# One list of events for both products of a graph layer, across its batch norm

## The chip, the cores and the metric

The kernel runs on one core of one Trainium2 chip. The metric is the device time of an execution in microseconds; the time before is the median of five executions, 1886.87 us (1885.16 to 1887.32). One further execution was taken with the profiler; it took 1887.02 us, of which the profile's span is 1885.1 us.

## The reference

Four graph layers follow each other on `x` of 128 x 64 x 256 (batch, nodes, features). Each is `x + layer(relu(layernorm(x)))`. The change is in layer 1:

```python
def _L1_gnn_ref(features, A, W1, b1, g1, be1, W2, b2, g2, be2):
    def _batchnorm(x, gamma, beta):
        mu = jnp.mean(x, axis=0)
        var = jnp.var(x, axis=0)
        return (x - mu) * jax.lax.rsqrt(var + EPS) * gamma + beta
    ...
    agg = jnp.einsum('nm,bmd->bnd', A_hat, features)
    x = agg.reshape(-1, d)
    h = jax.nn.relu(_batchnorm(x @ W1.T + b1, g1, be1))
    out = h @ W2.T + b2
    out = _batchnorm(out, g2, be2)
    return out.reshape(b, n, -1)
```

`W1` takes 256 features to 512, `W2` takes 512 back to 256. A batch norm's mean and variance run over all 8192 rows (128 x 64). So no channel of `h` is known before the first product is done for all rows of that channel.

## The kernel before

**Tiling.** Channels lie on the 128 partitions, rows on the free axis. The 8192 rows are cut into 16 tiles of 512 (`NS = 16`), which are worked on in 8 pairs. The 512 channels of `h` are four chunks of 128, numbered 0 to 3. A tile's chunks 0 and 1 lie in buffers called `hS` or `hT`, chunks 2 and 3 in buffers called `z`; `zslot(s, c)` gives the place of tile `s`, chunk `c`.

**Seven products for eight.** A 2 x 2 block product is done with seven block products (Strassen's way). For this a pair's four blocks b11, b21 (first tile) and b12, b22 (second tile) are used as they are and in differences T1, T2, T4, and a third one written over b12 (called T3 here). Products 1 to 7 are collected in three PSUM banks a, b and c; for instance `product("a", 4)` multiplies by T4 and adds into bank a. A bank is then evicted by ACT (with the bias) or added by DVE to what stands in SBUF already. Bank a is read off step by step, after each of products 1, 6, 7 and 4, which are added into it in this order.

**The first product** (`half`, matmul at L905) is done once for each pair and each half `g` of the output: half 0 makes chunks 0 and 1, half 1 makes chunks 2 and 3. Its order is written out by hand: each step is put into a list with a due time (`at(t, ...)`), the list is sorted, and the steps are issued in that order. All engines work off their own part of this order, first come first. Beside it run the preparation of later tiles (transposes L541, layer norm statistics L564 to L572, aggregation L585, sums L810). `evict` is L910, `add` L913, `stats` (the batch norm's partial statistics) L916. PSUM is split into a pool "gates" of five banks for the product and "rest" of three for the preparation.

**The batch norm's coefficients** (`bn_coeffs`, L857 to L863) are worked out for two chunks at once after each half of the last pair: DVE aggregates the statistics (L857) and adds epsilon (L859), POOL takes the power -1/2 (L860), and DVE does two multiplications and a subtraction (L861 to L863).

**The second product** (`second_product`, matmul at L1015) has a list of its own, sorted and issued after all of the first product. Each pair has 14 matmuls of the program: seven products with `k` = 0 (chunks 0 and 1) and `k` = 1 (chunks 2 and 3), both added into the same bank. In the trace each such matmul has two records. ACT applies the scale, shift and ReLU to each block (L991; four of the first pair's operations are on DVE, L987 and L989), DVE makes the sums of `k` = 0 and POOL those of `k` = 1 (L999 to L1005, both on DVE for the first pair), ACT evicts (L1019), DVE adds (L1022) and takes the second batch norm's statistics (L1028). All eight banks are one pool again. Between the two lists stand the closing of the preparation's memory and seven loads for later layers on SP's queue (L90).

Of the kernel before, what the change touches and what calls it, by code (L numbers as in the profile page):

```python
# [9 lines left out]
F32 = mybir.dt.float32  # L10
AF = mybir.ActivationFunctionType
ALU = mybir.AluOpType
AX = mybir.AxisListType

P = 128
# [5 lines left out]
def kernel(ctx: ExitStack, tc: tile.TileContext, a: dict, out: bass.AP):  # L21
# [60 lines left out]
    def bank(pool="psum"):  # L82
        return banks[pool][1].tile([P, 512], F32, tag="ps", name="ps")
# [4 lines left out]
    def load_const(name, src, shape, pool=const, queue=nc.sync):  # L88
        t = pool.tile(shape, F32, tag=name, name=name)
        queue.dma_start(t, src)  # L90
        return t
# [12 lines left out]
    nc.gpsimd.memset(ones, 1.0)  # L104
    mhalf = const.tile([P, 8], F32, tag="mhalf", name="mhalf")
    nc.gpsimd.memset(mhalf, -0.5)

    def block_diag(name, src):
        t = first.tile([P, P], F32, tag=name, name=name)
# [489 lines left out]
    def at(t, fn, *args):  # L599
        events.append((t, len(events), fn, args))  # L600
# [251 lines left out]
    def bn_coeffs(pool, co, stats, c0, c1, prm, name):  # L852
# [9 lines left out]
        nc.vector.tensor_mul(shift, mv[:, :, 0], scale)  # L862
        nc.vector.tensor_sub(shift, prm[:, 2, c0:c1], shift)  # L863

    co1 = const.tile([P, 3, HC], F32, tag="co1", name="co1")
    co2 = const.tile([P, 3, KC], F32, tag="co2", name="co2")

# [3 lines left out]
    with tc.tile_pool(name="pz", bufs=1, reuse_waits="tile") as pz:  # L871
# [13 lines left out]

        new_banks(gates=5, rest=3)
        GATE = 8.7
        events = []

        def at(t, fn, *args):  # L890
# [2 lines left out]
        def half(i, g):  # L893
            t0, r = GATE * (2 * i + g), {}
            z = {(n, o): zslot(2 * i + n, 2 * g + o) for n in range(2) for o in range(2)}

            def product(name, j):
                new = name not in r
                if new:
                    r[name] = bank("gates")  # L900
                (b11, b21), (b12, b22) = ([firsts[2 * i + n]["ag"][:, c, :] for c in range(KC)]
                                          for n in range(2))
                t1, t2, t4 = firsts[0]["t"]
                x_ = (b11, b21, b22, t4, t1, t2, b12)[j - 1]
                nc.tensor.matmul(r[name], con["w1"][:, OF[j], g, :], x_, start=new,  # L905
                                 stop=(name, j) in (("a", 4), ("b", 3), ("c", 2)), skip_group_check=True)

            def evict(n, o, name):
                m = 2 * g + o
                nc.scalar.activation(z[n, o], r[name], AF.Identity, bias=con["bn1"][:, 0, m : m + 1])  # L910

            def add(n, o, name):
                nc.vector.tensor_add(z[n, o], z[n, o], r[name])  # L913

            def stats(n, o):
                nc.vector.bn_stats(st1[:, 2 * g + o, 2 * i + n, :], z[n, o])  # L916

            for t, name, j in ((0, "c", 2), (1.72, "a", 1), (3.46, "b", 5), (4.32, "a", 6),
                               (6.07, "b", 3), (6.93, "a", 7), (GATE + 0.86, "a", 4)):
                at(t0 + t, product, name, j)  # L920
            for t, fn, n, o, name in ((2.75, evict, 0, 0, "a"), (3.5, add, 0, 0, "c"),
                                      (4.5, evict, 1, 1, "b"), (5.35, evict, 1, 0, "a"),
                                      (7.1, add, 1, 0, "b"), (7.95, add, 1, 1, "a"),
                                      (GATE + 1.9, evict, 0, 1, "a")):
                at(t0 + t, fn, n, o, name)
            for t, n, o in ((5.5, 0, 0), (9.0, 1, 0), (9.7, 1, 1), (GATE + 2.9, 0, 1)):
                at(t0 + t, stats, n, o)
            if i == NS // 2 - 1:
                at(t0 + GATE + 3, bn_coeffs, lns, co1, st1, 2 * g, 2 * g + 2, con["bn1"], "bn1")

        for i in range(NS // 2):
            for g in range(2):
# [22 lines left out]
                at(t2 + (1.7, 2.3, 4.2, 4.8)[q], f.stats, q)  # L955
            at(t2 + 5.4, f.root)

        for _, _, fn, args in sorted(events, key=lambda e: e[:2]):
            fn(*args)
        new_banks(psum=8)  # L960
        front.close()
        last.close()
        late = ctx.enter_context(tc.tile_pool(name="late", bufs=1, side="right", reuse_waits="tile"))
        adj4 = load_const("adj4", parts_d, [P, 4, P], late)
        adj3, smask = adj4[:, 0:3, :], adj4[:, 3, :]
        wl2 = [weight(f"wl2_{k}", a["W"][k], late) for k in range(3)]
        bl2 = row_bcast("bl2", a["bias"], D, late)
        wqk = late.tile([P, KC, D], F32, tag="wqk", name="wqk")
        aqk = late.tile([P, 7, P], F32, tag="aqk", name="aqk")
        wvo = late.tile([P, KC, D], F32, tag="wvo", name="wvo")  # L970
        wqkv = weight("wqkv", a["Wqkv"], late)
        wo = weight("wo", a["Wo"], late)

        events = []

        def second_product(i, tp):


            t0 = 7.0 * i
            tt, banks = {}, {}  # L980

            def z(n, c):
                return zslot(2 * i + n, c)

            def relu(n, c):
                if i == 0 and n == 1 and c % 2 == 0:
                    nc.vector.tensor_scalar(z(n, c), z(n, c), co1[:, 0, c : c + 1],  # L987
                                            co1[:, 1, c : c + 1], op0=ALU.mult, op1=ALU.add)
                    nc.vector.tensor_scalar_max(z(n, c), z(n, c), 0.0)  # L989
                else:  # L990
                    nc.scalar.activation(z(n, c), z(n, c), AF.Relu, bias=co1[:, 1, c : c + 1],  # L991
                                         scale=co1[:, 0, c : c + 1])

            def sums(name, k, engine):
                if name != "T3" and name not in tt:
                    tt[name] = tp.tile([P, 2, SUP], F32, tag=name, name=name)
                b11, b21, b12, b22 = (z(n, 2 * k + c) for n in range(2) for c in range(2))
                if name == "T1":
                    engine.tensor_sub(tt["T1"][:, k], b12, b11)  # L999
                elif name == "T2":  # L1000
                    engine.tensor_sub(tt["T2"][:, k], b22, tt["T1"][:, k])
                elif name == "T3":
                    engine.tensor_sub(b12, b22, b12)
                else:
                    engine.tensor_sub(tt["T4"][:, k], b21, tt["T2"][:, k])  # L1005

            def product(name, j, ks=(0, 1)):
                new = name not in banks
                if new:
                    banks[name] = bank()  # L1010
                for k in ks:
                    x_ = (z(0, 2 * k), z(0, 2 * k + 1), z(1, 2 * k + 1),
                          *(tt[v][:, k] if v in tt else None for v in ("T4", "T1", "T2")),
                          z(1, 2 * k))[j - 1]
                    nc.tensor.matmul(banks[name], w2[:, OF[j], k, :], x_, start=(new and k == 0),  # L1015
                                     stop=(k == 1), skip_group_check=True)
# [11 lines left out]
                nc.vector.bn_stats(st2[:, o, 2 * i + n, :], y(n, o))  # L1028

            def at(t, fn, *args):  # L1030
                events.append((t0 + t, len(events), fn, args))

            for k, (n, c) in enumerate(((0, 1), (0, 0), (0, 3), (0, 2), (1, 0), (1, 2), (1, 1), (1, 3))):
                at((-6.3, -5.8, -5.3, -4.4, -3.9, -3.4, -2.4, -1.9)[k], relu, n, c)
            for k, engine in enumerate((nc.vector, nc.gpsimd if i else nc.vector)):
                for name, t in (("T1", -2.8), ("T2", 0.1), ("T3", 0.6), ("T4", 1.6)):
                    at(t, sums, name, k, engine)
            for t, name, j in ((0, "c", 2), (1, "a", 1), (3, "b", 5), (5, "a", 6), (9, "a", 7),
                               (11, "b", 3), (13, "a", 4)):
                if i == 0 and t < 2:  # L1040
                    at(t, product, name, j, (0,))
                    at(t + 1.1, product, name, j, (1,))
                else:
                    at(t, product, name, j)
            at(2.2, lambda: evict(y(0, 0), 0, "a"))
            at(3.1, lambda: add(y(0, 0), y(0, 0), "c"))
            at(3.6, stats, 0, 0)
            at(4, lambda: evict(y(1, 1), 1, "b"))
            at(6, lambda: evict(tt["T2"][:, 0], 0, "a"))
            at(10, lambda: add(y(1, 1), y(1, 1), "a"))  # L1050
            at(10.5, stats, 1, 1)
            at(12, lambda: add(y(1, 0), tt["T2"][:, 0], "b"))
            at(12.5, stats, 1, 0)
            at(14.2, lambda: evict(y(0, 1), 1, "a"))
            at(15, stats, 0, 1)

        with tc.tile_pool(name="tp", bufs=2, reuse_waits="tile") as tp:
            for i in range(NS // 2):
                second_product(i, tp)
            for _, _, fn, args in sorted(events, key=lambda e: e[:2]):  # L1060
                fn(*args)
        bn_coeffs(lns, co2, st2, 0, KC, con["bn2"], "bn2")


# [354 lines left out]
```

## Time and profile before

| | |
|---|---|
| median of 5 executions | 1886.87 us |
| the profiled execution | 1887.02 us |
| its span | 1885.1 us |
| PE busy | 1859.7 us (99%) |
| DVE busy | 1137.1 us (60%) |
| ACT busy | 923.2 us (49%) |
| POOL busy | 643.2 us (34%) |

Times within the span are counted from its start. The last pair's first half of the first product begins at 1343.7, the second product ends at 1460.7. Busy time by stretch, in us:

| stretch | length | PE | DVE | ACT | POOL | granted clock |
|---|---|---|---|---|---|---|
| 1343.7 to 1356.7, last pair of the first product | 13.00 | 13.00 | 10.42 | 6.09 | 0.70 | 1.00 |
| 1356.7 to 1372.0, the seam | 15.30 | 11.97 | 13.52 | 10.32 | 1.11 | 0.78 |
| 1372.0 to 1390.0, second product | 18.00 | 18.00 | 15.91 | 15.13 | 12.02 | 1.00 |
| 1390.0 to 1460.9, second product | 70.90 | 70.90 | 51.31 | 39.85 | 29.26 | 1.00 |
| 1460.9 to 1475.0, second batch norm, into layer 2 | 14.10 | 10.17 | 10.98 | 6.51 | 8.29 | 1.00 |

How to read the profile: each engine has rows of instructions with start, duration, line, operation, output and inputs, and in square brackets how long the engine stood idle before and what released it. PEld is the weight load, which runs ahead of the matmul (PE). In the table by stretch of the profile the columns are the stretch, its length, busy time and number of instructions of PE, PEld, DVE, ACT and POOL, then the granted TensorE clock, the share of the DMA engines and GB/s. Where an instruction waits for several things, the profile names the one that came last by its own clock, which can be a neighbour in time rather than the true cause. In a group's row the numbers behind the bar are busy us and mean ns of one instruction.

### The profile page before, as it was taken

Reading aid. Unit: us, or ns where it says so; the run is one execution under the profiler, and the core shown is the slowest. Engines: PE = TensorE matmul, PEld = TensorE weight load, DVE = VectorE, ACT = ScalarE, POOL = GpSimd, SP = SyncE. Lnnn points to the kernel's source line nnn. Section 1 sums busy time; section 2 is a strip of 40 time slices with the busy share of each in tenths; the row PEclk is TensorE's granted clock in tenths of the full one; section 3 lists DMA queues with packets and bytes.
Section 4 is the critical chain, followed back from the end, with each engine's and each line's share of the span. In section 5 each row is a group of like instructions: output and inputs, shape, how many; then the busy total and the mean of one; then the engine's idle time right before and its main releaser. Section 6 shows DMA issues by size and latency. Waiting matters only on the chain.

```text
span 1885.1 us, 19823 instructions
## 1 busy us (share of the span) xinstructions
PE 1859.7 (99%) x7080; PEld 1171.1 (62%) x7080; DVE 1137.1 (60%) x2268; ACT 923.2 (49%) x1591; POOL 643.2 (34%) x527
## 2 busy tenths in 40 slices
PE   8999999999999999999999999999999999999999
PEld 7997444444445666666444444556444788888887
DVE  6775777634546445435633333588787776677774
ACT  6775666534435335433533333478574344433442
POOL 4451422543324442422432222377253312211220
PEclk9999999999999999999999999999999999999999
DMA  5110001000001000000000000233200111111100
GB/s 145 57 57 0 1 1 34 12 1 0 1 0 45 1 0 1 1 1 15 8 0 1 1 0 22 101 112 112 70 1 1 46 45 45 35 46 45 46 23 34
DMA packets 50641, 54.85 MB, mean 29 GB/s; under 512 B 3184, under 2 KB 45936, under 8 KB 50544
## 3 DMA queue, kind: packets, MB, share of 16 engines
q1 hardware_dynamic: 50080, 53.40, 9.1%
q8 instruction: 56, 0.92, 0.2%
q14 instruction: 41, 0.34, 0.1%
q10 hardware_dynamic: 464, 0.20, 0.0%
HBM read 36.55 MB, written 17.04 MB: 28 GB/s over the span
## 4 chain that ended last, share of the span: by engine, by line
PE 94%; DVE 3%; ACT 1%; POOL 1%; DMA 1%; issue 0%; SPq 0%; DVEq 0%; POOLq 0%
PE ps L665 34%; PE ps L671 19%; PE ps L1185 8%; PE ps L1015 5%; PE ps L905 5%; PE ps L1250 3%; PE ps L367 3%; PE ps L357 3%; PE ps L396 2%; PE ps L1226 2%; PE ps L1173 2%; PE ps L1260 2%; PE ps L1291 1%; PE ps L585 1%; PE ps L1198 1%; PE ps L541 1%
## 5 line engine op out<-in xcount | busy, mean ns | idle before, releaser
L687 DVE TENSOR_TENSOR gate<-gate,ps 128x512 f32<-128x512 f32 (+2 forms) x378 | 223.9, 620 | 446.9 <-PE ps L671 367.4
L665 PE MATMUL ps<-tx,wih 128*128 128x512 f32 (+2 forms) x1008 | 446.9, 542 | 2.7 <-ACT gate L690 1.0
L665 PE MATMUL ps<-hT,wih 128*128 128x512 f32 (+2 forms) x756 | 338.5, 541 | 0.0
L690 ACT COPY gate<-ps 128x512 f32<-128x512 f32 (+2 forms) x252 | 134.3, 533 | 378.6 <-PE ps L671 325.4
L665 PEld LDWEIGHTS ps<-tx,wih 128*128 128x128 f32 x1008 | 190.5, 190 | 193.3 <-issue 130.1
L683 ACT ACTIVATE gate<-gate,lbias 128x512 f32<-128x512 f32 (+2 forms) x252 | 216.7, 860 | 160.2 <-DVE gate L687 160.2
L671 PE MATMUL ps<-h,whh 128*128 128x512 f32 (+2 forms) x576 | 256.6, 527 | 0.0
L665 PEld LDWEIGHTS ps<-hT,wih 128*128 128x128 f32 x756 | 143.6, 190 | 141.6 <-issue 79.4
L671 PE MATMUL ps<-th,whh 128*128 128x512 f32 (+2 forms) x432 | 192.4, 527 | 0.0
L710 POOL TENSOR_TENSOR gate<-gate 128x1024 f32<-128x1024 f32 (+2 forms) x36 | 71.9, 2019 | 297.6 <-ACT gate L683 297.6
L1185 PE MATMUL ps<-wl,ag 128*128 128x256 f32 x768 | 172.1, 380 | 0.0
L671 PEld LDWEIGHTS ps<-h,whh 128*128 128x128 f32 x576 | 109.4, 190 | 100.2 <-issue 76.5
L1185 PEld LDWEIGHTS ps<-wl,ag 128*128 128x128 f32 x768 | 143.4, 190 | 20.2 <-ACT ag L1178 1.8
L710 POOL TENSOR_TENSOR cell<-gate 128x1024 f32<-128x1024 f32 (+2 forms) x36 | 79.4, 2227 | 175.2 <-ACT gate L683 175.2
L1141 POOL TENSOR_TENSOR ln_rn<-ln_rn,mhalf 128x4 f32<-128x4 f32 (+1 forms) x33 | 32.8, 993 | 300.8 <-DVE ln_rn L1140 300.3
L671 PEld LDWEIGHTS ps<-th,whh 128*128 128x128 f32 x432 | 82.1, 190 | 75.2 <-issue 57.4
L1148 ACT ACTIVATE h<-x,ln_rn 128x256 f32<-128x256 f32 x128 | 68.2, 593 | 103.0 <-DVE ln_rn L1144 103.0
L710 POOL TENSOR_TENSOR cell<-gate,cell 128x1024 f32<-128x1024 f32 (+2 forms) x32 | 65.2, 2055 | 110.2 <-ACT gate L683 110.2
L690 DVE COPY gate<-ps 128x512 f32<-128x512 f32 (+2 forms) x126 | 78.6, 624 | 20.8 <-PE ps L671 20.8
L715 ACT ACTIVATE gate<-cell 128x1024 f32<-128x1024 f32 (+2 forms) x72 | 68.1, 952 | 27.1 <-POOL cell L710 27.1
L683 ACT ACTIVATE gate<-ps,lbias 128x512 f32<-128x512 f32 (+2 forms) x126 | 79.5, 631 | 3.8 <-PE ps L671 1.0
L627 DVE TENSOR_TENSOR tx<-hT,tx 128x512 f32<-128x512 f32 (+2 forms) x72 | 59.1, 820 | 14.9 <-PE ps L665 10.2
(227 smaller groups left out, 2932.5 us busy)
## 6 DMA issues: line engine op xcount, KB each, us to landing
xt<-in_x_dram SPq DMA_DIRECT2D x30, 512.0 KB, 4.2
x1d<-xt SPq DMA_DIRECT2D x16, 512.0 KB, 3.0
x<-x1d SPq DMA_DIRECT2D x16, 512.0 KB, 5.2
out_dram<-x SPq DMA_DIRECT2D x15, 512.0 KB, 3.0
wih<-in_WihT_dram SPq DMA_DIRECT2D x16, 256.0 KB, 5.0
whh<-in_WhhT_dram SPq DMA_DIRECT2D x12, 256.0 KB, 4.9
xt<-in_x_dram SPq DMA_DIRECT2D x8, 128.0 KB, 4.0
wl<-in_W_dram SPq DMA_DIRECT2D x3, 256.0 KB, 4.3
```

Of the source, the lines that this page charges most:

```text
L627: yield nc.vector.tensor_sub(t[k], *((b[1][0], b[0][0]), (b[1][1], t[0]), (b[1][1], b[1][0]), (b[0][1], t[1 % len(t)]))[k])
L665: nc.tensor.matmul(wide(p_[:, :N]), wih[0][:, OF[k], gi, :], x_, start=first_, stop=(j == 0), skip_group_check=True)
L671: nc.tensor.matmul(p_[:, :N], whh[0][:, OF[k], gi, :], h_, start=False, stop=True, skip_group_check=True)
L683: nc.scalar.activation(to, r[bank_][:, :N] if bank_ else to, fn, bias=lbias[:, l, m : m + 1])
L687: nc.vector.tensor_add(slot(n, hc), slot(n, hc), r[bank_][:, :N])
L690: op(slot(n, hc), r[bank_][:, :N])
L710: fn(*((t["G"] if isinstance(t, dict) and "G" in t else st["c"])[:, n, :, : st["N"]] for t in tiles))
L715: nc.scalar.activation(o_, c, AF.Tanh)
L905: nc.tensor.matmul(r[name], con["w1"][:, OF[j], g, :], x_, start=new, stop=(name, j) in (("a", 4), ("b", 3), ("c", 2)), skip_group_check=True)
L1015: nc.tensor.matmul(banks[name], w2[:, OF[j], k, :], x_, start=(new and k == 0), stop=(k == 1), skip_group_check=True)
L1148: nc.scalar.activation(v[tag][:, q, :], v[src][:, q, :], AF.Relu, bias=v["rn"][:, 1, q : q + 1], scale=v["rn"][:, 0, q : q + 1])
L1185: nc.tensor.matmul(v["W"][:, q, :], v["ag"][:, c, m, ts(2 * k + q, P)], wl2[m][:, c, :], start=(n == 0), stop=(n == 3 * KC - 1))
```

## The change

1. **One list.** Layer 1's second product puts its events into the same list as the first. `emit(B + 18.0)` issues all that is due up to then, `B` being the due time of the last pair's start; then the memory is closed and the seven loads are issued as before, and `emit(1e9)` issues the rest.
2. **Coefficients by chunk.** `bn_coeffs1(c)` works out one chunk: DVE aggregates, POOL does the other five steps on one column (add a new constant `eps`, power, two multiplications, a subtraction). It is issued once for each of the four chunks, each after its last statistics.
3. **Early products.** For pairs 0 and 1 the matmuls of a1, b5 and c2 with `k` = 0, which need only chunks 0 and 1, are issued before those with `k` = 1; they come right behind the first product's last matmul. Their T1 with `k` = 0 lies in a tile `early` that is taken from the preparation's memory. The order of ReLUs, sums and evictions of these two pairs is written out anew. Of pair 0's ReLUs one is on DVE (second tile, chunk 1); the two that were there (second tile, chunks 0 and 2) are on ACT.
4. **Two bank pools.** The pools of five and three banks stay through the second product: even pairs take "rest", odd pairs "gates". The pool of eight is made after it.
5. **Due times** of the last pair of the first product are closer together (its second half starts 6.02 after its first, not 8.7). The order of PE's own matmuls in that pair stays as it was.
6. **Sums.** T3 is made before T2, and T2 is T3 + b11 in place of b22 - T1, the same value up to rounding. For pair 1 the sums with `k` = 1 are on POOL as before; pair 0's stay on DVE.

```diff
+    eps = const.tile([P, 1], F32, tag="eps", name="eps")
+    nc.gpsimd.memset(eps, EPS)
...
+    def bn_coeffs1(c):
+
+        mv = lns.tile([P, 2], F32, tag=f"bn1mv{c}", name="bn1mv", bufs=1)
+        nc.vector.bn_aggr(mv, st1[:, c, :, :].rearrange("p s k -> p (s k)"))
+        scale, shift, v = (co1[:, k, c : c + 1] for k in range(3))
+        nc.gpsimd.tensor_add(v, mv[:, 1:2], eps)
+        nc.gpsimd.tensor_tensor(v, v, mhalf[:, :1], ALU.pow)
+        nc.gpsimd.tensor_mul(scale, v, con["bn1"][:, 1, c : c + 1])
+        nc.gpsimd.tensor_mul(shift, mv[:, 0:1], scale)
+        nc.gpsimd.tensor_sub(shift, con["bn1"][:, 2, c : c + 1], shift)
...
+            end = i == NS // 2 - 1
+            if end:
+                t0 = B + 6.02 * g
+            late_a = 6.1 if g else 6.9
...
-            if i == NS // 2 - 1:
-                at(t0 + GATE + 3, bn_coeffs, lns, co1, st1, 2 * g, 2 * g + 2, con["bn1"], "bn1")
+            if end:
+                at(t0 + (7.9 if g else 7.35), bn_coeffs1, 2 * g)
+                at(t0 + 9.2, bn_coeffs1, 2 * g + 1)
...
-        for _, _, fn, args in sorted(events, key=lambda e: e[:2]):
-            fn(*args)
-        new_banks(psum=8)
...
+            def sum_of(name, k):
+                if name == "T1" and k == 0 and i < 2:
+                    if i == 0 and not early:
+                        e = pb[0].tile([P, Q, D], F32, tag="xt", name="early")
+                        early.append(e.rearrange("p (n q) d -> p n (q d)", n=2))
+                    return early[0][:, i]
+                if name not in tt:
+                    tt[name] = tp[0].tile([P, 2, SUP], F32, tag=name, name=name)
+                return tt[name][:, k]
...
-                elif name == "T2":
-                    engine.tensor_sub(tt["T2"][:, k], b22, tt["T1"][:, k])
...
+                elif name == "T2":
+                    engine.tensor_add(sum_of("T2", k), b12, b11)
...
-                    banks[name] = bank()
+                    banks[name] = bank("gates" if i % 2 else "rest")
...
+            if i < 2:
+
+                for t, name, j in (((12.9, "a", 1), (13.76, "b", 5), (14.6, "c", 2)) if i == 0 else
+                                   ((15.5, "a", 1), (16.3, "c", 2), (17.2, "b", 5))):
+                    at_us(t, product, name, j, (0,))
+                for t, n, c in (((11.0, 0, 0), (11.8, 1, 0), (13.0, 0, 1), (17.0, 0, 2), (17.6, 0, 3),
+                                 (18.5, 1, 2), (19.3, 1, 3)) if i == 0 else
+                                ((14.4, 0, 0), (15.2, 0, 1), (16.0, 1, 0), (20.9, 0, 3), (21.6, 0, 2),
+                                 (23.5, 1, 2), (24.3, 1, 1), (25.1, 1, 3))):
+                    at_us(t, relu, n, c)
+                if i == 0:
+                    at_us(17.4, relu, 1, 1, True)
...
+                for t, name, j in (((18.06, "a", 1), (18.92, "c", 2), (19.78, "b", 5)) if i == 0 else
+                                   ((22.4, "c", 2), (23.2, "a", 1), (25.8, "b", 5))):
+                    at_us(t, product, name, j, (1,))
...
+        for i in range(NS // 2):
+            second_product(i)
+        emit(B + 18.0)
         front.close()
         last.close()
...
+        with tc.tile_pool(name="tp", bufs=2, reuse_waits="tile") as tp_:
+            tp.append(tp_)
+            emit(1e9)
+        new_banks(psum=8)
         bn_coeffs(lns, co2, st2, 0, KC, con["bn2"], "bn2")
```

## The prediction, made before the result was known

> **What bounds the kernel now.** The page first: PE is busy 1859.7 of 1885.1 us, so a change can only win where PE waits or runs slowly. The diff touches the seam of layer 1 where the first product (L905) ends, the batch norm takes its coefficients, and the second product (L1015) begins; so next the chain of waits, in order of time, over that seam:
>
> ```profile
> 1343.85 9.16 PE ps L905 x20
> ...
> 1355.44 5.84 DMA wqkv<-in_Wqkv_dram
> 1361.28 2.91 PE ps L1015 x3
> ```
>
> PE carries both sides, and between them stands a DMA whose data the first second-product matmul doesn't read. Which wait is it really? The timelines of PE and of its weight loads:
>
> ```profile
> 1354.74 2.07 PE L905 MATMUL ps<-ag,w 128*128 128x512 f32 x4
> 1358.66 1.12 PE L905 MATMUL ps<-T,w 128*128 128x512 f32 x2 [1.85 <-DVE z L913]
> 1361.26 3.78 PE L1015 MATMUL ps<-hS,w 128*128 128x512 f32 x4 [1.48 <-DMA wqkv<-in_Wqkv_dram]
> 1364.84 3.18 PE L1015 MATMUL ps<-z,w 128*128 128x512 f32 x4
> 1367.86 3.60 PE L1015 MATMUL ps<-T,w 128*128 128x512 f32 x8
> ...
> 1361.26 0.50 PEld L1015 LDWEIGHTS ps<-hS,w 128*128 128x128 f32 x2 [2.31 <-ACT hS L991]
> ```
>
> The weight load names the true releaser, the ReLU on ACT (the wqkv DMA merely ended then). Eight matmuls in 3.60 us are the normal pace: 0.43 us from one start to the next, two records to one product with one k, so 0.86 us for it. The eight from 1361.28 to 1367.86 took 0.82 each. The stretches say why:
>
> ```profile
> 1356.60:1358.60 2.00, 0.21 (x1) 0.00 (x0) 1.97 (x5) 0.00 (x0) 0.00 (x0) 1.00 0.89 227
> ...
> 1361.20:1363.00 1.80, 1.74 (x2) 0.84 (x3) 1.14 (x4) 0.71 (x2) 0.55 (x1) 0.50 0.47 151
> ...
> 1368.00:1370.00 2.00, 2.00 (x6) 0.75 (x5) 2.00 (x4) 2.00 (x5) 0.00 (x0) 1.00 0.00 0
> ```
>
> The column before the last two is the granted clock: 1.00, then 0.50, then 1.00. The loss at the seam: PE's last ordinary L905 work ends at about 1356.63 (last start 1356.2 plus 0.43); the next 46 records (2 of L905, and the 22 single-k products of the first two pairs) should take 46 x 0.4295 = 19.76 us, but the third pair's first matmul starts at 1383.31: 26.68 us. So **6.92 us are lost**: a wait of 2.03 for a z sum on DVE, one of 1.76 for the ReLU, and 8 x (0.82 - 0.43) = 3.14 at half clock. This is nearly all that the change can win.
>
> DVE shows why the z sum is late:
>
> ```profile
> 1353.51 1.02 DVE L857 BATCH_NORM_AGGREGATE bn1mv<-st 128x2 f32<-128x96 f32 x2
> 1354.56 0.17 DVE L859 TENSOR_SCALAR co<-bn1mv 128x2 f32<-128x2 f32 x1
> 1355.54 0.16 DVE L861 TENSOR_TENSOR co<-co,bn 128x2 f32<-128x2 f32 x1 [0.81 <-POOL co L860]
> ...
> 1357.34 1.27 DVE L913 TENSOR_TENSOR z<-z,ps 128x512 f32<-128x512 f32 x2
> ```
>
> DVE works out the coefficients of the first two channel chunks, standing still for POOL's power, with the sums that PE needs queued behind.
>
> **The change, step by step.** I lay the changed program's order on each engine over the times above. Products are named by bank and number as in the code (a4 = product 4 into a); "pair 0, a1 k0" is one single-k product.
>
> **Coefficients to POOL.** DVE keeps only the four aggregates (0.5 each); per chunk POOL gets five steps on one column. Rows: a small multiply 0.20, a one-column power 0.55, 0.08 between dependent steps:
>
> ```profile
> L572 POOL TENSOR_TENSOR ln_rn<-ln_rn 128x4 f32<-128x4 f32 x16 | 3.3, 206 | 1.3
> L175 POOL TENSOR_TENSOR deg<-deg,mhalf 128x1 f32<-128x1 f32 x1 | 0.5, 546 | 0.0
> ```
>
> One chunk: 4 x 0.20 + 0.55 + 4 x 0.08 = 1.67 us. POOL is otherwise idle here (20.3 us before its first power), so nothing is queued behind. Chunk 0 aggregates by 1352.05, so its coefficients stand at about 1353.8; chunk 1 (1354.05) at 1355.9.
>
> **The last L905 products.** DVE is now free when a7 of the last half is done: sum at 1356.84 (its weight load at 1355.68 plus the 1.16 us of the same step one half earlier), ending 1357.53. a4 starts at 1357.55, not 1358.66. PE waits 0.92 instead of 2.03.
>
> **Early products in the gap.** ACT does three ReLUs (0.80, one per 0.70) from 1355.55, in the 4.19 us in which it stood idle: 1356.35, 1357.06, 1357.77. Behind them on ACT is the eviction of a4, which cannot start before 1358.7: no harm. The first early T1 (DVE, 0.69) ends at 1358.14. So at 1358.41 PE goes straight from a4 into pair 0's a1, b5, c2 with k0, then pair 1's a1, c2, b5 (ReLUs 1360.1 to 1361.5, T1 at 1362.25), until 1363.57. No wait among the six.
>
> **Chunks 2 and 3.** a4's eviction ends 1359.4. Chunk 2's aggregate ends at 1359.8, POOL 1361.55; chunk 3's aggregate at 1360.85, POOL starts at 1361.6. Here DVE runs five operations in a row (a difference, the two-step ReLU, T3, T2) until about 1364.4, and POOL meets them. The trace has this meeting once:
>
> ```profile
> 1226.18 2.49 DVE L635 TENSOR_TENSOR hT<-gate 128x512 f32<-128x512 f32 x4
> 1226.28 1.46 POOL L571 TENSOR_TENSOR ln_rn<-ln_rn,mhalf 128x4 f32<-128x4 f32 x1 [4.97 <-DVE ln_rn L570]
> 1227.82 0.31 POOL L572 TENSOR_TENSOR ln_rn<-ln_rn 128x4 f32<-128x4 f32 x1
> ```
>
> The power took 1.46 where its usual is 1.02, the small one 0.31 for 0.20, and DVE lost nothing. By this row chunk 3 pays 0.44 + 4 x 0.11 = 0.88: ready at 1364.15. The Trainium skill speaks against the change here: "SBUF — State Buffer", section "SBUF: two separate sides", holds that a VectorE operation with two SBUF inputs and a GpSimd operation take one port pair exclusively, the later one blocked for a whole instruction. With strict turns the five steps end at about 1365.7. Floor 1363.3 (no meeting), ceiling 1365.7; I take the row, since it is this very pair of operations.
>
> From there: ReLU of z(0,3) 1364.2 to 1365.0, so pair 0's c2 k1 starts at 1365.05 (PE ready at 1364.43: waits 0.62); ReLU of z(1,2) to 1365.7, T1 to 1366.45, so b5 k1 at 1366.5 (waits 0.60). T1's new wait for pair 1's b5 k0 (they share memory) was over at 1363.8. The next six products find their operands ready (ACT's evictions by 0.4 us). Pair 1's a6 k1 needs T3 and T2 from POOL in turn with DVE: ready 1376.6 against 1376.0, 0.65 waited (between 0 and 0.75: POOL's rows here are 1.27 or 1.72). The third pair starts at 1379.2.
>
> **The clock.** With at most 0.92 idle at once I expect 1.00 throughout; after the second batch norm, at 1460.9 to 1475.0, PE was busy only 10.17 of 14.10 us and the clock stayed 1.00. The skill, "TensorE: Matmul & The Clock Gate", section "What's actually happening", lowers the clock after an idle window of about 3.4 us; our gaps were 2.03 and 1.76 with 0.86 of work between, so by a strict reading the clock should not have fallen, and closing them should not return the 3.14. The row shows that it fell right after them: I follow the row. By the rule alone the gain would be 3.14 less.
>
> **The rest.** The two bank pools: an even pair's a takes the bank that the pair two before leaves with its last DVE sum, three slots of 1.72 earlier; DVE meets those sums within 0.4 us of PE now, so that hides it. T2 from T3 instead of T1 is the same count, later by one DVE step (1.75), with some 8 us before its use. After the last pair the transposes wait for a DVE sum that ended 0.8 us before them in this trace. The one added memset is at the start, where POOL waits anyway. SP's seven loads keep their places and released waits.
>
> **Sum.** Lost after: 0.92 + 0.62 + 0.60 + 0.65 = 2.79, against 6.92: **4.1 us won**. The profiled execution took 1887.02 (span 1885.1 and 1.9 around it), so 1882.9; the median of the runs is 1886.87, so 1882.8.
>
> **Rivals.**
> - *POOL and DVE don't disturb each other*: chunk 3 at 1363.3, one wait of 0.36 in place of 0.62 and 0.60. Gain 5.0 (5.6 if a6 needn't wait): 1881.5. For: power and multiply keep 1.02 and 0.20 in all 15 other places. Against: the row at 1226. Chance 0.20.
> - *Full blocking*, chunk 3 at 1365.7: 1.55 later than by the row, so gain 2.5, 1884.3, within the noise. For: the page, and DVE differences of 1.77 beside POOL. Against: the row. Chance 0.11.
> - *The clock falls all the same*: gain 1.0, 1885.9. Against: 0.92 idle. Chance 0.03.
> - *Slower: POOL's one-column steps are dear.* Four chains of five steps in one queue now gate everything. At 1.0 us a step (the 128x4 power) a chain takes 5.3: chunk 1 at 1362.7 holds ACT's ReLU, behind it the eviction of a4, and chunk 3 comes at 1373.3, 9.1 later than I have it: 5.0 lost, 1891.9. It turns to a loss from about 0.75 us a step, which POOL takes for 256 columns; the 0.20 of four columns speaks against it. Chance 0.06.
>
> **Numbers.** The forecast case has 0.60, its own range 1882.0 to 1883.8. Two in ten left out: 1880.8 to 1885.6. A measurement of this kernel tells about 0.2% (3.8 us) from no change. My case lies just beyond, some 0.8 of it counts as faster, with the first rival 0.68; nearly all of the rest is same.
>
> **What would show it.** Right: a4 at about 1357.5; six L1034 products of the two first pairs between 1358.4 and 1363.6 without a gap; the granted clock 1.00 from 1356 to 1370; L872 to L876 at 0.2 to 0.3 us with a power of 0.55 (up to 1.0 in chunk 3); the third pair's first matmul at about 1379. Wrong: a clock of 0.5, POOL steps of 0.6 or more, PE waits for a bank in later pairs, or a pair period other than 12.04 us.

## The result, and the profile after

The changed kernel takes 1882.82 us (median of 30 executions, 1880.74 to 1883.97); beside it, on the same chip, the kernel before takes 1886.07 us (50 executions, 1884.76 to 1888.06). The ratio taken over all executions is 0.9981, 95% interval 0.9976 to 0.9986; the medians alone differ by **3.25 us**, 0.17%. The profiled execution took 1881.2 us (span 1879.5).

| profiled execution | before | after |
|---|---|---|
| span | 1885.1 | 1879.5 |
| last pair's first matmul of the first product | 1343.69 | 1341.40 |
| third pair's first matmul of the second product | 1383.31 | 1377.66 |
| **between them, "the seam"** (also "the stretch") | **39.62** | **36.26** |
| granted clock from 1356.7 to 1372.0 | 0.78 | 1.00 |

The seam gives 3.36 us, which agrees with the medians. The spans differ by 5.6; the other 2.3 are not the change's. About 0.76 lie in two waits of PE for ACT near 17.6 and 20.6 us, and 1.53 in the granted clock at another place, near 1231 us, to which the last section returns. A second profile of the changed kernel (`after_5`, below) has both again, with a seam of 36.25.

The timeline of PE after the change, in the rows that answer to those shown of before:

```profile
1355.30 1.12 PE L919 MATMUL ps<-T,w 128*128 128x512 f32 x2 [0.78 <-DVE z L927]
1356.27 1.02 PE L1034 MATMUL ps<-hS,w 128*128 128x512 f32 x2
1357.12 1.02 PE L1034 MATMUL ps<-early,w 128*128 128x512 f32 x2
1357.98 2.74 PE L1034 MATMUL ps<-hS,w 128*128 128x512 f32 x6
1360.56 1.02 PE L1034 MATMUL ps<-early,w 128*128 128x512 f32 x2
1361.42 1.02 PE L1034 MATMUL ps<-z,w 128*128 128x512 f32 x2
1363.31 1.12 PE L1034 MATMUL ps<-z,w 128*128 128x512 f32 x2 [0.87 <-ACT z L1002]
1364.74 2.84 PE L1034 MATMUL ps<-T,w 128*128 128x512 f32 x6 [0.31 <-DVE T L1018]
...
1374.98 2.84 PE L1034 MATMUL ps<-T,w 128*128 128x512 f32 x6 [0.39 <-POOL T L1022]
```

The first row is a4. The next four are the six early products, without a gap. Then four waits remain in all: before a4, before pair 0's c2 with `k` = 1 (1363.31), before its b5 (1364.74), and before pair 1's a6 (1374.98). From one start to the next, less 0.86 for each pair of records, they cost 0.95 (from 1354.35, when PE is free), 1.03, 0.57 and 0.55. Another 0.46 goes in small pieces: about 0.1 behind the first, third and fourth wait (a4 to the next start: 0.97 for 0.86), and 0.14 around the matmul at 1370.89, before which the profile names no wait. Together 3.56 us are lost now, where 6.92 were.

The table by stretch, with the clock in the column before the last two:

```profile
1356.70:1372.00 15.30, 14.12 (x33) 5.77 (x32) 11.17 (x18) 11.66 (x17) 5.70 (x12) 1.00 0.17 65
1361.20:1363.00 1.80, 1.24 (x3) 0.19 (x1) 1.13 (x2) 0.56 (x1) 1.13 (x2) 1.00 0.00 0
```

PE is busy 14.12 of 15.30 us here, against 11.97 before, with the full clock throughout. (The changed kernel reaches the seam 2.3 us earlier, so the same times take in a somewhat later part of its work.)

What holds the largest wait, at 1363.31? The chain of waits (start, us, what) shows little but POOL's small steps and gaps of 0.04 to 0.08 between them, then a ReLU:

```profile
1359.45 1.04 POOL co L873
...
1360.56 0.40 POOL co L874
...
1361.03 0.65 POOL co L875
1361.77 0.65 POOL co L876
...
1363.16 0.81 ACT z L1002
```

The steps are those for the coefficients of chunk 3. The ReLU in the chain is the one that T1, and so b5, waits for. PE's wait at 1363.31 ends with the ReLU before it, the first of three in ACT's timeline, which start when POOL is done:

```profile
1362.44 2.22 ACT L1002 ACTIVATE z<-z,co 128x512 f32<-128x512 f32 x3 [2.36 <-POOL co L876]
```

The timelines of POOL, for comparison two of chunk 2's steps and then the last four of chunk 3's, and of DVE at the same time:

```profile
1358.51 0.19 POOL L874 TENSOR_TENSOR co<-co,bn 128x1 f32<-128x1 f32 x1
1358.78 0.19 POOL L875 TENSOR_TENSOR co<-bn1mv,co 128x1 f32<-128x1 f32 x1
...
1359.45 1.03 POOL L873 TENSOR_TENSOR co<-co,mhalf 128x1 f32<-128x1 f32 x1
1360.56 0.39 POOL L874 TENSOR_TENSOR co<-co,bn 128x1 f32<-128x1 f32 x1
1361.03 0.65 POOL L875 TENSOR_TENSOR co<-bn1mv,co 128x1 f32<-128x1 f32 x1
1361.76 0.65 POOL L876 TENSOR_TENSOR co<-bn,co 128x1 f32<-128x1 f32 x1
```

```profile
1359.30 0.69 DVE L1018 TENSOR_TENSOR early<-hS 128x512 f32<-128x512 f32 x1 [0.58 <-ACT hS L1002]
1359.91 0.54 DVE L998 TENSOR_SCALAR hS<-hS,co 128x512 f32<-128x512 f32 x1
1360.48 0.43 DVE L1000 TENSOR_SCALAR hS<-hS 128x512 f32<-128x512 f32 x1
1360.94 0.69 DVE L1020 TENSOR_TENSOR hS<-hS 128x512 f32<-128x512 f32 x1
1361.67 0.69 DVE L1022 TENSOR_TENSOR T<-hS 128x512 f32<-128x512 f32 x1
```

Add start and duration in both. L874 on POOL ends at 1360.95, DVE's L1000 at 1360.91. L875 ends at 1361.68, DVE's L1020 at 1361.63. L876 ends at 1362.41, DVE's L1022 at 1362.36. Each small step ends 0.04 to 0.05 after the DVE operation that was running when it began. Whether that is a rule is tested below.

### The profile page after: what moved, and what is told of

The parts are those of the page before. It is cut to its first block, busy times and chain, and to the rows that moved or that the text cites. A ratio compares the mean times of both kernels' runs of the same rounds, so it can differ in the third digit from the quotient of the medians.

```text
span 1879.5 us, 19837 instructions
## 1 busy us (share of the span) xinstructions
PE 1855.6 (99%) x7080; PEld 1169.4 (62%) x7080; DVE 1129.4 (60%) x2258; ACT 923.9 (49%) x1592; POOL 647.0 (34%) x546
## 4 chain that ended last, share of the span: by engine, by line
PE 93%; DVE 3%; POOL 1%; ACT 1%; issue 1%; DMA 0%; ACTq 0%; DVEq 0%; SPq 0%; POOLq 0%
PE ps L667 34%; PE ps L673 19%; PE ps L1256 8%; PE ps L919 4%; PE ps L1034 4%; PE ps L359 3%; PE ps L369 3%; PE ps L1321 3%; PE ps L398 2%; PE ps L1244 2%; PE ps L1297 2%; PE ps L1331 2%; PE ps L1362 1%; PE ps L587 1%; PE ps L1269 1%; PE ps L543 1%
```

## The experiments

By the prediction two parts of the change each win, the early products by filling PE's waits and the coefficients on POOL by freeing DVE; and nearly half of the old loss was the clock. Each of the three was then tried apart.

**The coefficients alone** (`coeffs_alone`). The kernel before, with `bn_coeffs1` (and its constant) from the changed kernel, and the call:

```diff
-                at(t0 + GATE + 3, bn_coeffs, lns, co1, st1, 2 * g, 2 * g + 2, con["bn1"], "bn1")
+                at(t0 + 9.6, bn_coeffs1, 2 * g)
+                at(t0 + GATE + 3, bn_coeffs1, 2 * g + 1)
```

> The kernel before with one part of the change: layer 1's coefficients by chunk, five steps on POOL; no early products, no bank pools. The seam is measured from the first matmul of the last pair's first product to the first matmul of the third pair's second product: 39.62 us before, 36.26 after. My theory (the early products carry the gain, because they are the only work that can stand in PE's wait for chunks 2 and 3): a4 starts about 1.1 us earlier, and PE waits that much longer for the first ReLUs and for chunks 2 and 3; seam 38.5 to 40.0, the granted clock still falls to 0.5, time the same as before. Rival (the coefficients carry it, by freeing DVE): seam 37.5 or less, 1882.5 to 1884.

Measured: 1886.4 us, ratio 1.0 (0.9992 to 1.0009); seam 39.66 us. PE's timeline:

```profile
1356.04 1.12 PE L918 MATMUL ps<-T,w 128*128 128x512 f32 x2 [0.78 <-DVE z L926]
1358.64 1.98 PE L1029 MATMUL ps<-hS,w 128*128 128x512 f32 x4 [1.48 <-ACT hS L1005]
1362.83 3.67 PE L1029 MATMUL ps<-z,w 128*128 128x512 f32 x4 [2.21 <-ACT z L1005]
```

a4 comes 1.07 us earlier, as foreseen (13.90 after the seam's start, 14.97 before). But a third wait of 2.21 takes the place: chunk 3's coefficients stand at 19.79 after the seam's start, against 20.04 before, so all that hangs on them is nearly as late as ever. Beside DVE's own ReLUs and T1 the chain of five steps took 2.61 here, where it takes 1.62 alone. Taken alone this part wins nothing.

**All but the coefficients** (`early_alone`). The changed kernel, with the coefficients again in twos by the old `bn_coeffs`. The early products stay, and with them the one list, the bank pools, the due times and the new order of ReLUs and sums:

```diff
-                at(t0 + (7.9 if g else 7.35), bn_coeffs1, 2 * g)
-                at(t0 + 9.2, bn_coeffs1, 2 * g + 1)
+                at(t0 + 9.2, bn_coeffs, lns, co1, st1, 2 * g, 2 * g + 2, con["bn1"], "bn1")
```

> The changed kernel with the old coefficients (two chunks at once, DVE with the power on POOL); early products, one list and bank pools stay. My theory: a4 is late again (waits about 2.0 instead of 0.95), but chunks 2 and 3 stand earlier than in the changed kernel, since DVE's small steps don't queue on POOL or meet DVE there; b5 with k1 waits little. The two cancel: seam 36 to 37, clock 1.00, the time of the changed kernel within 1 us. Rival (the coefficients on POOL are half of the gain): seam 37.5 to 38.5.

Measured: 1884.01 us, ratio 0.9987 (0.9981 to 0.9994); seam 36.60 us. These parts together carry 3.02 of the 3.36 at the seam, and 2.4 us in the medians. PE's row of a4:

```profile
1357.28 1.13 PE L919 MATMUL ps<-T,w 128*128 128x512 f32 x2 [1.85 <-DVE z L927]
```

The profile's other waits are 0.32 before pair 1's early T1 and, as in the changed kernel, 0.39 before its a6; the wait for chunk 3, 0.87 in the changed kernel, is gone: with DVE doing most of it, chunk 3's coefficients stand 5.08 us after a4's start (7.11 in the changed kernel). So moving the coefficients wins about 1 us at a4 and loses most of it again at chunk 3. In the kernel before, two products with `k` = 0 stood ahead of PE's wait for chunks 2 and 3; here six do. That the four more are what wins is the plain reading of the rows; the other parts of this run were not taken apart.

**The clock alone** (`fillers`). The kernel before, with two idle matmuls (four records in the trace) into a spare bank in each of PE's two waits. Nothing reads that bank, and no work of the kernel is left out.

```diff
+        def filler():
+            ps = bank("rest")
+            for k in range(2):
+                nc.tensor.matmul(ps, con["w1"][:, 0, 0, :], firsts[NS - 2]["ag"][:, 0, :], start=True, stop=True)
+
+        at(GATE * (NS - 1) + 8.0, filler)
+        at(GATE * (NS - 1) + GATE + 2.0, filler)
```

> The kernel before with four idle matmuls, two before a4 and two behind it, into a bank that nobody reads; they do no work for the result and stand only in PE's two waits at the seam. It measures the clock by itself. My theory: the clock stays 1.00 at the seam, the eight slow records take 0.43, but PE then meets the ReLUs of chunks 2 and 3 that the slow clock had hidden, so of the 3.14 us only about 1.5 are won: seam 37.9 to 38.6, time about 1.5 us below the kernel before. Rival (the full price of the clock as I predicted it): seam 36.5. Rival (idle matmuls don't count for the clock): seam 39.6 or more, clock 0.5.

Measured: 1886.67 us, ratio 0.9999 (0.9991 to 1.0008); seam 39.60 us. A miss, and the most useful one. PE's timeline:

```profile
1356.68 1.88 PE L961 MATMUL ps<-ag,w 128*128 128x512 f32 x4
1358.69 1.12 PE L905 MATMUL ps<-T,w 128*128 128x512 f32 x2
1359.66 1.88 PE L961 MATMUL ps<-ag,w 128*128 128x512 f32 x4
1361.37 1.91 PE L1022 MATMUL ps<-hS,w 128*128 128x512 f32 x4
1364.67 1.98 PE L1022 MATMUL ps<-z,w 128*128 128x512 f32 x4 [1.39 <-ACT z L998]
...
1369.49 1.98 PE L1022 MATMUL ps<-T,w 128*128 128x512 f32 x4 [1.11 <-ACT hS L1026]
```

The fillers (L961) close both waits, and the second product's matmuls run at full pace (1.91 for four records, 3.78 before). What they gain, PE then waits: 1.39 for ReLUs of chunks 2 and 3, and 1.11 for an eviction of bank a that stands on ACT behind other ReLUs. In the kernel before, the slow matmuls covered these waits. Its weight loads show one of them, behind the first four slow records:

```profile
1364.64 0.54 PEld L1015 LDWEIGHTS ps<-z,w 128*128 128x128 f32 x2 [1.17 <-ACT z L991]
```

With the granted clock at 1.00 from 1356.7 to 1372.0, `fillers` ends where the kernel before ends. The half clock there cost nothing; the chain of DVE and ACT set the end.

**No ReLU on DVE** (`relu_act`). The changed kernel, with the ReLU of tile 1, chunk 1 of pair 0 on ACT:

```diff
-                    at_us(17.4, relu, 1, 1, True)
+                    at_us(17.4, relu, 1, 1)
```

> The changed kernel with the ReLU of pair 0, second tile, chunk 1 on ACT, between those of chunks 2 and 3, instead of two steps on DVE. It takes two of DVE's five operations out of the meeting with POOL's steps for chunk 3. My theory (DVE's operations hold POOL's chain up: 3.2 us for chunk 3 against 1.6 to 1.7 for the others): the chain takes 2.0 to 2.7, the waits of c2 k1 and b5 k1 (1.03 and 0.57) shrink by 0.5 to 1.0 in sum, seam 35.3 to 35.8. Rival (the chain is slow for another reason): the chain stays at 3.2, seam 36.3.

Measured: 1882.34 us, ratio 0.9973 (0.9963 to 0.9983); seam 35.41 us, 0.85 less than the changed kernel's (the median of these nine executions is not told apart from its median). Chunk 3's chain takes 2.37 us where it took 3.23: fewer meetings, an earlier end.

**Chunks 2 and 3 back on DVE** (`dve_half`). The changed kernel; chunks 0 and 1 stay on POOL one by one. For chunks 2 and 3 together, aggregates, add, multiplications and subtraction are on DVE again and only the power on POOL:

```diff
...
+                if g:
+                    at(t0 + 7.9, bn_coeffs1b, 0)
+                    at(t0 + 9.2, bn_coeffs1b, 1)
+                    at(t0 + 10.7, bn_coeffs1b, 2)
+                else:
+                    at(t0 + 7.35, bn_coeffs1, 0)
+                    at(t0 + 9.2, bn_coeffs1, 1)
...
```

> The changed kernel, with the coefficients of chunks 2 and 3 worked out together and by the old division of labour: two aggregates, one add, two multiplications and a subtraction on DVE, only the power (two columns) on POOL; chunks 0 and 1 stay on POOL, chunk by chunk. The stretch counted is that from the last pair's first matmul of half 1 ... here: from the first matmul of the last pair's first product to the third pair's first matmul of the second product (36.26 us in the changed kernel, 39.62 before). Theory: chunk 3's chain on POOL (3.23 us beside five DVE operations) is what pair 0's c2 k1 (1.03 waited) and b5 k1 (0.57) wait for; with one POOL step in place of ten the coefficients of both chunks stand about 1 us earlier: c2 k1 waits under 0.3, stretch 35.0 to 35.6. Rival: DVE is as tight there as POOL, and its four added steps of 0.16 with a wait of 0.8 for the power give the same time back: stretch 36.1 to 36.7.

Measured: 1881.61 us, ratio 0.997 (0.9959 to 0.9981); seam 35.01 us. PE's timeline from pair 1's last early product on:

```profile
1362.91 1.02 PE L1056 MATMUL ps<-early,w 128*128 128x512 f32 x2
1363.77 1.92 PE L1056 MATMUL ps<-z,w 128*128 128x512 f32 x4
1365.84 2.84 PE L1056 MATMUL ps<-T,w 128*128 128x512 f32 x6 [0.15 <-DVE T L1040]
```

The wait for chunk 3 is gone (1.92 for four records), that for b5 shrinks to 0.15. Of the splits run, the best goes by what stands beside the steps: POOL where DVE runs statistics, DVE for chunks 2 and 3, where POOL's steps would meet its differences.

**A ReLU earlier on ACT, and everything at once** (`relu_reorder`, `combo2`). `relu_reorder` is `relu_act` with one more edit; `combo2` is that, `dve_half`'s edit, and pair 0's a1 ahead of a4:

```diff
-                                 (23.5, 1, 2), (24.3, 1, 1), (25.1, 1, 3))):
+                                 (23.5, 1, 2), (24.3, 1, 1), (23.9, 1, 3))):
```

> The changed kernel with two edits: the ReLU of tile 1, chunk 1 of pair 0 on ACT (as in relu_act, 35.41 us for the stretch), and the ReLU of tile 1, chunk 3 of pair 1 issued one place earlier on ACT, so that POOL's T3 of pair 1 may start earlier. Theory: the wait of 0.55 before pair 1's a6 with k = 1 comes from POOL's T1, T3, T2 in a row starting late behind that ReLU; it shrinks to under 0.2, stretch 34.9 to 35.1. Rival: that wait comes from DVE and POOL taking turns for T3 and T2, whatever the start: it stays at 0.4 or more, stretch 35.3 to 35.6.

> The changed kernel with all of these: dve_half's coefficients for chunks 2 and 3, relu_reorder's two edits on ACT, and pair 0's a1 with k = 0 issued ahead of the last pair's a4, so that it fills the wait of 0.95 before a4. Theory: the waits have separate causes and their removal adds up: stretch 34.0 to 34.8, median 1.5 to 2.2 us under the changed kernel's. Rival: as when PE alone was filled (fillers, nothing won), DVE's and ACT's queue sets the end: removing waits one by one only moves them, stretch 35.2 or more.

Measured: 1882.69 us (0.9982, 0.9975 to 0.9989) with a seam of 36.54, and 1882.67 us (0.998, 0.9973 to 0.9987) with 36.83. For `relu_reorder` theory and rival both missed: against `relu_act` the one more edit loses 1.13. For `combo2` the theory missed; its seam lies where the rival put it (35.2 or more), but PE's largest wait there is the same one as in `relu_reorder`, 1.51. Rows of `relu_reorder`, POOL and then DVE:

```profile
1370.59 1.28 POOL L1020 TENSOR_TENSOR z<-z 128x512 f32<-128x512 f32 x1
1371.94 1.59 POOL L1022 TENSOR_TENSOR T<-z,z 128x512 f32<-128x512 f32 x1
```

```profile
1370.60 1.81 DVE L1020 TENSOR_TENSOR hS<-hS 128x512 f32<-128x512 f32 x1 [2.31 <-ACT hS L1002]
1372.44 1.64 DVE L1022 TENSOR_TENSOR T<-hS 128x512 f32<-128x512 f32 x1
```

POOL starts its T3 earlier, but now beside DVE's T3, which starts 0.01 later and ends 0.54 after POOL is done. The two take turns from there on. In `relu_act` the same DVE operations took 1.16 and 0.69. ACT's eviction of bank a, which overwrites what T2 reads, waits 2.90 for DVE, and PE 1.51 for the eviction. Here it is DVE that loses.

**PE's wait before a4 filled** (`dve_half_a1`), **and repeats** (`dve_half_5`, `after_5`). The edit on `dve_half` is one number:

```diff
-                for t, name, j in (((12.9, "a", 1), (13.76, "b", 5), (14.6, "c", 2)) if i == 0 else
+                for t, name, j in (((12.0, "a", 1), (13.76, "b", 5), (14.6, "c", 2)) if i == 0 else
```

> dve_half (stretch 35.01 us, median 1881.6) with one edit: pair 0's a1 with k = 0 is issued ahead of the last pair's a4 and fills the wait of 0.95 before it. Theory, now that fillers and combo2 have shown that work put into a PE wait isn't won where another chain sets the end: chunks 2 and 3 hang on a4, its eviction, statistics and the coefficients, and that chain starts no earlier, so PE arrives 0.86 earlier at pair 0's c2 k1 and waits for it instead: stretch 34.7 to 35.1. Rival: PE's own row is the bound here, and the filled wait is won whole: stretch 34.1 to 34.3.

> dve_half once more, with more rounds, on the same chip and beside the same runs as the changed kernel. Theory: its 1.25 us at the stretch show in the median: 1881.0 to 1881.9, ratio to before 0.9970 to 0.9976. Rival: the earlier 1881.61 of seven runs was luck, and it lies at the changed kernel's 1882.8.

> The changed kernel itself, beside the two others. Stretch 36.2 to 36.4, median 1882.4 to 1883.0. After the 2.48 us wait for a DVE sum at the seam of layers 0 and 1 (about 1231) the clock may be half or full: three of the first six profiles with that wait, before the last three, showed half; if it is a matter of chance, full and half both come, whatever the kernel.

Measured, side by side on one chip: `dve_half_a1` 1881.68 us (0.9975, 0.9965 to 0.9985), seam 35.01; `dve_half_5` 1881.69 us (0.9975, 0.9964 to 0.9985), seam 35.00; the changed kernel 1883.01 us (0.998, 0.9972 to 0.9988), seam 36.25. PE's timeline of `dve_half_a1`:

```profile
1354.51 1.02 PE L1056 MATMUL ps<-hS,w 128*128 128x512 f32 x2
1355.45 1.12 PE L936 MATMUL ps<-T,w 128*128 128x512 f32 x2
1356.41 1.02 PE L1056 MATMUL ps<-early,w 128*128 128x512 f32 x2
1357.27 2.77 PE L1056 MATMUL ps<-hS,w 128*128 128x512 f32 x6
1360.19 1.12 PE L1056 MATMUL ps<-early,w 128*128 128x512 f32 x2
1361.50 1.98 PE L1056 MATMUL ps<-z,w 128*128 128x512 f32 x4 [0.18 <-ACT z L1024]
```

A wait of 0.95 is filled with useful work and not a hundredth is won: the six records from 1357.27 are done in 2.58, and the next start, 1360.19 with pair 1's early T1, is 0.34 later than that; the one after it, 1361.50, waits for a ReLU of chunks 2 and 3, which hang on a4. The best version run is `dve_half`, with or without this edit; it beats the changed kernel by 1.25 us at the seam in both profiles and by 1.3 in the median, though the two intervals overlap.

**The rule of the meeting** (`no_meet`). `relu_act`, with DVE's T3 and T2 behind an operation that itself waits for chunk 3:

```diff
...
-                for t, name, k in (((12.6, "T1", 0), (18.4, "T3", 0), (19.0, "T2", 0), (19.6, "T1", 1),
+                for t, name, k in (((12.6, "T1", 0), (19.7, "T3", 0), (19.8, "T2", 0), (19.6, "T1", 1),
...
```

> relu_act with DVE's T3 and T2 (k = 0) of pair 0 issued behind its T1 with k = 1, which waits for chunk 3's coefficients; so of the five DVE operations beside chunk 3's chain on POOL only pair 1's early T1 (two operands in SBUF) is left. Theory, read off the profiles so far: a POOL step that starts while DVE runs an operation with two operands in SBUF, or one of the two-step ReLU, stands until that one operation ends (a multiplication ends 0.04 to 0.05 after it, the power 0.42 to 0.49 after it), and is not slowed beside DVE's statistics, aggregates or sums with an operand in PSUM. Then only the power is held: 0.94 as in relu_act, all four small steps 0.19, chain 2.0 to 2.1 us (2.37 in relu_act, 3.23 in the changed kernel). Rival: the price belongs to the step or to the queue: the last step takes 0.55 as in relu_act, chain 2.3 to 2.4. The stretch is not the point, since pair 0's a6 now waits for T2: 35.4 to 36.3 us (35.41 in relu_act).

Measured: one execution, 1883.26 us beside 1885.22 of before; seam 36.22, with a new wait of 1.04 for an eviction, as the delayed T2 makes likely. POOL's timeline for chunk 3, and the only DVE operation that runs beside it:

```profile
1361.47 0.94 POOL L873 TENSOR_TENSOR co<-co,mhalf 128x1 f32<-128x1 f32 x1
1362.50 0.19 POOL L874 TENSOR_TENSOR co<-co,bn 128x1 f32<-128x1 f32 x1
1362.77 0.19 POOL L875 TENSOR_TENSOR co<-bn1mv,co 128x1 f32<-128x1 f32 x1
1363.03 0.19 POOL L876 TENSOR_TENSOR co<-bn,co 128x1 f32<-128x1 f32 x1
```

```profile
1361.32 0.69 DVE L1018 TENSOR_TENSOR early<-hS 128x512 f32<-128x512 f32 x1 [0.58 <-ACT hS L1002]
```

The chain is 2.01 us (1361.21 to 1363.22), in the theory's 2.0 to 2.1, not the rival's 2.3. Only the power, which began beside the early T1, was held: it ends at 1362.41, 0.40 after T1.

## Why the prediction was right, and where it was not

- **The total.** The forecast was 1882.8, the measured median 1882.82. The agreement is better than the reasoning: the forecast gain was 4.1 us and 3.25 came, and the five executions that it was reckoned from lie 0.8 above the 50 taken later. The gain is just under the 0.2% that was called no change; the interval of these runs, 0.05% to each side, tells it from none all the same.
- **The wait at a4**: 0.92 forecast, 0.95 measured. The cause is shown: with the coefficients back on DVE (`early_alone`) the profile has 1.85 idle before it, for 0.78.
- **The six early products** run without a gap, as laid out. With all the rest but the coefficients they carry the gain (`early_alone`: 3.02 of 3.36).
- **One chain of five POOL steps**: 1.67 forecast, 1.63 measured (1349.98 to 1351.61), so the slower rival falls: a step costs 0.19, not 0.75.
- **Chunk 3 beside DVE is the step that failed.** "By this row chunk 3 pays 0.44 + 4 x 0.11 = 0.88" took the excess of one meeting for a price per step. The chain was 3.23, an excess of 1.56 over 1.67. Counted from the seam's start, it began 0.13 earlier than laid out and ended 0.55 later, and c2 waited 1.03 for 0.62. The row could have told it: of DVE's four operations of 0.68 from 1226.18 the third ended near 1228.07 (an estimate: the row merges the four, and evenly spaced they overlap by some 0.07 each), and POOL's 0.31 ended at 1228.13. Read in this way it was not slowed by 0.11; it stood until that operation was done, which happened to be near.
- **The rule weighed there.** The Trainium skill, "SBUF — State Buffer", section "SBUF: two separate sides", was set aside for the row; it names which DVE operations hold the port pair (two SBUF inputs, or a two-port mode), and on this the runs agree. Steps that began beside the differences L1018 to L1022 or the two-step ReLU were held to their end; beside L930, L870 and the sums L927 with a PSUM operand they kept 0.19. The other direction does not show with such small steps: in `dve_half` DVE's T1 starts 0.30 into a POOL power of 0.70 and keeps its 0.69. The sum made from the rule, 1365.7, stands without its working and came out too late: the first step began ahead of DVE's T1 and kept 0.19, a held multiplication ends 0.04 to 0.05 after the DVE operation, and a held power 0.40 to 0.49 after it. So the "full blocking" rival (gain 2.5) had the mechanism and the forecast was nearer in size: chunk 3 stood 7.11 after a4's start, forecast 6.60, full blocking 8.15. The rival without disturbance (gain 5.0) is refuted.
- **b5 and a6**: 0.57 and 0.55 measured, 0.60 and 0.65 forecast. The small pieces behind and between the waits, 0.46 in all, were not counted. The terms close: 2.79 + 0.03 + 0.41 - 0.03 - 0.10 + 0.46 = 3.56.
- **The clock** stayed at 1.00, and the rival in which it falls is out. But the price of 3.14 was no price: `fillers` has the full clock and gains nothing. The 6.92 was right as a total of what PE lost, and wrong as a list of separate gains. For the same reason the weighing of the clock rule ("by the rule alone the gain would be 3.14 less") says nothing of the gain: at full clock the kernel before has the same seam (39.60 for 39.62). What a half clock would cost in the changed kernel, no run shows.
- **The costs put at nothing** (bank pools, T2 from T3, the memset, SP's loads) show nowhere in the rows read: the changed kernel is 5.65 ahead at the third pair (1377.66 for 1383.31) and still 5.65 ahead when PE leaves the second product (1454.91 for 1460.56). None was tried alone.

## What to carry to other kernels

A slow or waiting PE is worth its lost time only if nothing else is late right behind it: fill the wait with idle work first, and see whether the end moves. When small POOL steps meet DVE, look at what DVE runs there: beside operations with two SBUF operands price each step to the end of the DVE operation, beside statistics at nothing. Moving real work into a wait wins only as long as PE, and not another engine's chain, is late behind it: the early products ahead of chunks 2 and 3 won, and one of them moved ahead of a4 as well won nothing more.

## What had not been expected of the hardware

**The clock falls by chance after one and the same wait.** At the seam of layers 0 and 1, which the change doesn't touch, PE waits 2.47 to 2.49 us for a DVE sum in every profile. The changed kernel, in the first profile and in `after_5`:

```profile
1230.48 1.12 PE L919 MATMUL ps<-T,w 128*128 128x512 f32 x2 [2.47 <-DVE hS L927]
```

```profile
1231.57 2.07 PE L919 MATMUL ps<-T,w 128*128 128x512 f32 x2 [2.47 <-DVE hS L927]
```

The two records took 1.12 in one and 2.07 in the other. These two, or in `dve_half` the ones right behind them, ran slowly in 7 of the 13 profiles (before, `fillers`, `relu_act`, both of `dve_half`, `after_5`, `no_meet`; granted clock 0.83 from 1230 to 1240) and at full pace in six (1.00); the same program shows both. It is worth about 1.5 us, so two single profiles can differ by half of what this change wins. The skill, "TensorE: Matmul & The Clock Gate", section "What's actually happening", has the activity window run free of the program, which fits the chance; its idle window of about 3.4 us is longer than this wait, and why 2.47 can be enough stays open.

**A large meeting costs DVE.** Beside POOL's small steps DVE kept its 0.69, 0.54 and 0.43. Beside a POOL operation on 512 columns that began first, its difference took 1.16 to 1.81 and ended 0.54 to 0.55 after POOL's (`relu_act`, `relu_reorder`).
